# Rotary attention: a tile's three projections traced in one step of the loop, and layer-norm statistics traced over more steps

## The chip, the cores and the metric

The program runs on one core of a Trainium2 chip. The metric is the device time of one execution in microseconds (us), as the median of several runs. The engines are named as in the profile: PE is TensorE's matmul stream, PEld its weight loads, DVE is VectorE, ACT is ScalarE, POOL is GpSimd and SP is SyncE. Each engine works through its own list of instructions in order and waits at semaphores for the others.

## The reference

The whole program is a stack of four pairs of gated layers: a cross-attention-like layer and a feed-forward layer, each applied to a layer norm of the running activations `x` of shape (32, 64, 256), and added back through `tanh` of a gate. All of it is float32 at the interface. The change concerns the last cross-attention layer, `L3_xattn`, which is cut here to what matters:

```python
x = x + jnp.tanh(g_xattn[3]) * _L3_xattn_ref(_layernorm(x), ctx_2048, Wq, bq, Wk, bk, Wv, bv, Wo, bo)

def _L3_xattn_ref(x, c, ...):          # x, c: (32, 64, 256): 64 channels, 256 positions
    q = split_heads(_proj(x, Wq, bq))  # 8 heads of 8 channels
    k = split_heads(_proj(c, Wk, bk))
    v = split_heads(_proj(c, Wv, bv))
    q = _apply_rotary(q_emb, q)        # t * cos(pos) + rot(t) * sin(pos)
    k = _apply_rotary(k_emb, k)
    scores = jnp.einsum('bhtc,bhsc->bhts', q, k) / math.sqrt(K_CH)
    p_attn = jax.nn.softmax(scores, axis=-1)
    out = jnp.einsum('bhts,bhsc->bhtc', p_attn, v)
    return _proj(out.transpose(...).reshape(...), Wo, bo)
```

Keys and values come from the context, queries from the layer norm of `x`.

## The kernel before

The activations stay on the chip in one tile `c.x` of 16 row tiles of 128 x 256. Each row tile holds two of the 32 sequences. `program` runs the eight layers as Python generators, `block0` to `block7`, and interleaves neighbouring ones: a step of one, then a step of the next. Block 6 is the rotary attention. Its first steps, g = 0 to 6, are traced between the last steps of block 5; from g = 7 it runs alone, with `weights7` (which prepares the last layer's weights on PE, ACT and POOL) traced between its steps from g = 60 on. Block 7, the last feed-forward layer, follows.

The order in which things are traced is not the order in which they run. A planner in the framework takes the traced program, treats the place in the trace as a priority, and plans every engine's list by costs that it assumes: an instruction that is ready in its plan may be placed ahead of earlier ones that are not. It also hands out buffers: a tile of a pool waits until an older tile of the same tag has been read for the last time. Block 7's statistics of `x`, for example, stand in VectorE's list through most of block 6, right behind each update of `x`.

Block 6 works in steps g = 0 to 139, four steps for each of the 32 sequences, so eight steps for a row tile. A step does parts of several sequences at different stages:

- `scores(w, p, g)`, in each step. For the sequence `p` that has just begun, a product `pp` of queries and keys (line 1219) of which only the maximum is kept, by a VectorE reduction (`mx`, line 1227). For the sequence `w` that began six steps earlier, the product again as `pw` (line 1211) with the maxima folded into the queries (`qs`), in the other orientation, and its exponential `e` on ScalarE (line 1223).
- `shift` (lines 1196 and 1198), four steps after a sequence began, turns the maxima and makes `qs`.
- `mix` (line 1234), after eight and ten steps, multiplies `e` with the values; `normalise` (lines 1245 to 1249) after eleven divides by the sums; `turn` (line 1254) after thirteen and `finish` (lines 1260 to 1263) after fifteen, once per row tile, apply the output weights and add to `c.x` on POOL.
- `start(i)` makes keys, values and queries of row tile i. `_norm` (line 139) makes the normalised `xn`. Keys: eight matmuls into `pp` (line 1161), two VectorE operations with cosine and sine (`t`, line 1164), then on POOL a sum `k` (line 1170) and two masked copies `kb` (line 1173). Queries: the same matmuls with `xn`, the same two operations, and a sum `q` on POOL (line 1177). Values: matmuls into `pv` (line 1181) and two ScalarE copies into `va` (line 1186).

[...] Two belong to `c.aux`, tag "a", for one-bank tiles. `pair(name)` hands out two-bank tiles: two buffers in the pool `ps2`, and a third, `c.third`, once block 5 has given its banks back; with the third, every third request goes to it. `pw`, `pp` and the key and query projections take a `pair`; `pv` takes a bank of `c.aux`.

For tile i = g // 8 + 1, `start` is a generator that is advanced at the end of three steps: at g % 8 = 1 (norm and keys), 5 (queries) and 7 (values). Tile 0 is made at g = 0 at once.

The layer-norm statistics of four row tiles form one group, `lns`. The first is made ahead of g = 0. Group n is traced from g = 32n - 14: a mean and variance of one tile in each of four steps (`_mean`, lines 98 and 101), and the inverse root (`_inverse`, `_rsqrt`, lines 87 to 108: eleven small VectorE operations, three Newton rounds among them) at once in the fifth.

## Time and profile before

| | |
|---|---|
| Median of 3 runs | 1457.77 us (1457.44 to 1458.16) |
| Profiled execution: time, span | 1453.52 us, 1451.70 us |
| Granted TensorE clock, mean over the span | 0.934 |
| Block 6: first and last score reduction start | 908.53 us, 1264.28 us |
| PE, DVE, ACT, POOL busy in that stretch of 355.7 us | 332.14, 244.09, 163.51, 113.56 us |

The profile is one execution. Its page gives, for each group of instructions, the line of the kernel, the engine, the operation, the tiles that it writes and reads, the busy time with the mean of one in ns, and then the time in which the engine sat idle just before it, with what ended that. The timeline gives instructions in order of time: start, length of the merged group, and in brackets the idle time before it and its releaser. A view of windows gives the busy time of PE, PEld, DVE, ACT and POOL in a stretch, then the granted TensorE clock, the share of DMA and the rate. The ends of matmuls are modelled, so a busy PE is not a PE at its peak; the time from one group's start to the next one's says more.

### The profile page before, as it was taken

How to read it: one execution, taken by the hardware profiler on the slowest of the kernel's cores; microseconds unless marked ns; L12 is line 12 of the kernel's file. 1: busy time of each engine (PE TensorE's matmuls, PEld its weight loads, DVE VectorE, ACT ScalarE, POOL GpSimd, SP SyncE). 2: the span in 40 equal slices, each digit the busy share in tenths (PEclk: the TensorE clock that was granted, in tenths of full speed). 3: DMA queues.
4: the chain of work that ended last, by engine and by line, in shares of the span. 5: the costliest groups of instructions: out<-in, count | busy, mean ns of one | idle time of the engine just before them, and what ended most of it. 6: DMA issues, size and time to landing. Idle time of an engine off the chain costs nothing.

```text
span 1451.7 us, 21390 instructions
## 1 busy us (share of the span) xinstructions
PE 1265.6 (87%) x8342; PEld 745.8 (51%) x8342; DVE 930.1 (64%) x2189; ACT 619.1 (43%) x1044; POOL 448.9 (31%) x466
## 2 busy tenths in 40 slices
PE   1889989999879999778888874899899899999999
PEld 1666445455223677555555552455455455546665
DVE  5679685643378877686888778677776677532111
ACT  2554451312311455566777762255455354531110
POOL 3352442301131323344555455233135332100000
PEclk9999999999999999887998887699899899999999
DMA  5000000100530200000000010200000000000000
GB/s 202 15 7 9 1 1 11 48 0 8 196 116 1 95 1 1 1 1 1 2 1 1 1 60 0 87 2 1 1 2 1 1 1 2 1 0 15 15 15 14
DMA packets 10293, 34.12 MB, mean 24 GB/s; under 512 B 1360, under 2 KB 5968, under 8 KB 8528
## 3 DMA queue, kind: packets, MB, share of 16 engines
q1 hardware_dynamic: 10192, 32.76, 6.3%
q8 instruction: 65, 1.06, 0.3%
q14 instruction: 36, 0.29, 0.1%
HBM read 30.66 MB, written 2.10 MB: 23 GB/s over the span
## 4 chain that ended last, share of the span: by engine, by line
PE 55%; DVE 25%; POOL 9%; issue 4%; ACT 4%; DMA 2%; SPq 0%; POOLq 0%; DVEq 0%; ACTq 0%
PE pw L1211 5%; PE po L1371 4%; PE pg L1361 4%; PE pu L1361 4%; PE pp L1219 4%; PE pc L581 4%; PE po L1234 3%; POOL kb L1173 2%; DVE mx L1227 2%; PE pq L806 2%; PE pu L434 2%; PE pg L434 2%; PE pm L1061 2%; PE pu L437 2%; DMA w<-in_l2f 2%
## 5 line engine op out<-in xcount | busy, mean ns | idle before, releaser
L1223 ACT ACTIVATE e<-pw 128x1024 f32<-128x1024 f32 x128 | 131.0, 1024 | 175.5 <-PE pp L1219 171.5
L1227 DVE TENSOR_REDUCE mx<-pp 128x4 f32<-128x1024 f32 x128 | 156.0, 1219 | 77.4 <-PE pp L1219 77.4
L1211 PE MATMUL pw<-qs,kb 32*128 32x256 f32 x1024 | 159.0, 415 | 7.0 <-DVE mx L1227 7.0
L1219 PE MATMUL pp<-kb,q 32*128 32x512 f32 x512 | 153.7, 676 | 7.5 <-DVE mx L1227 5.0
L1211 PEld LDWEIGHTS pw<-qs,kb 32*128 32x128 f32 x1024 | 88.3, 188 | 49.5 <-issue 26.6
L581 PE MATMUL pc<-xw,wb 64*64 64x512 f32 x768 | 93.3, 619 | 0.2 <-DVE x L514 0.2
L440 ACT ACTIVATE sg<-pg 128x512 f32<-128x512 f32 (+1 forms) x75 | 37.8, 511 | 115.9 <-PE pg L434 50.5
L98 DVE BATCH_NORM_STATS2 ln_st<-x 128x6 f32<-128x256 f32 x128 | 51.0, 411 | 38.2 <-POOL x L1263 27.6
L1364 DVE TENSOR_TENSOR h<-pu,sg 128x512 f32<-128x512 f32 x32 | 22.1, 691 | 80.8 <-PE pu L1361 80.8
L441 DVE TENSOR_TENSOR h<-pu,sg 128x512 f32<-128x512 f32 (+1 forms) x75 | 42.5, 573 | 48.3 <-PE pu L434 30.0
L1234 PE MATMUL po<-e,va 128*32 128x256 f32 x1024 | 70.6, 395 | 1.2 <-ACT e L1223 1.2
L1363 ACT ACTIVATE sg<-pg 128x512 f32<-128x512 f32 x32 | 19.1, 597 | 122.8 <-PE pg L1361 122.7
L732 POOL TENSOR_TENSOR acc<-acc,sq 128x512 f32<-128x512 f32 x28 | 39.4, 1408 | 69.8 <-ACT sq L731 68.4
L581 PEld LDWEIGHTS pc<-xw,wb 64*64 64x64 f32 x768 | 29.8, 138 | 59.6 <-issue 58.8
L1361 PE MATMUL pg<-xf,wa 128*128 128x512 f32 x128 | 60.3, 592 | 0.0
L1361 PE MATMUL pu<-xf,wa 128*128 128x512 f32 x128 | 60.3, 592 | 0.0
L1170 POOL TENSOR_TENSOR k<-t,t 128x512 f32<-128x512 f32 x16 | 20.3, 1266 | 123.4 <-DVE t L1164 123.4
L1371 PE MATMUL po<-hb,h 128*128 128x256 f32 x256 | 55.9, 379 | 0.0
L1066 POOL TENSOR_TENSOR v<-v,wb 128x512 f32<-128x512 f32 x32 | 40.6, 1274 | 42.7 <-ACT v L1065 42.5
L1371 PEld LDWEIGHTS po<-hb,h 128*128 128x128 f32 x256 | 48.6, 190 | 8.3 <-issue 1.9
L139 DVE TENSOR_SCALAR xn<-x,ln_mv,ln_r 128x256 f32<-128x256 f32 x112 | 49.5, 474 | 4.9 <-PE pt L153 4.1
L1219 PEld LDWEIGHTS pp<-kb,q 32*128 32x128 f32 x512 | 41.0, 192 | 22.4 <-DVE mx L1227 16.5
(337 smaller groups left out, 3012.8 us busy)
## 6 DMA issues: line engine op xcount, KB each, us to landing
w<-in_l2f SPq DMA_DIRECT2D x12, 512.0 KB, 4.4
wa<-in_l0f SPq DMA_DIRECT2D x2, 1828.0 KB, 12.2
wa<-in_l1f SPq DMA_DIRECT2D x2, 1536.0 KB, 9.2
wa<-in_l3f SPq DMA_DIRECT2D x2, 1536.0 KB, 8.1
wb<-in_conv SPq DMA_DIRECT2D x1, 2048.0 KB, 7.6
ctx<-in_ctxT SPq DMA_DIRECT2D x2, 1024.0 KB, 6.2
ctx<-in_ctxN SPq DMA_DIRECT2D x2, 1024.0 KB, 6.0
out<-x SPq DMA_DIRECT2D x16, 128.0 KB, 1.7
```

The lines of the kernel that those rows point to most:

```text
L98: ins = c.nc.vector.bn_stats(st, c.x[:, i, :])
L139: c.nc.vector.tensor_scalar(xn, c.x[:, i, :], mv[:, j, 0:1], rs[:, j : j + 1], ALU.subtract, ALU.mult)
L434: nc.tensor.matmul(p, wt[:, k, fc], xf[:, k, :N], start=k == 0, stop=False, skip_group_check=True)
L441: nc.vector.tensor_tensor(h[s][:, f, :], pu, sg, ALU.mult)
L581: nc.tensor.matmul(pcs[h][to], w[rows, k, m, h, :], xw[rows, k, h, :, Z - m : Z - m + 32], start=m == 0, stop=m == Z)
L1211: nc.tensor.matmul(pw[:, jj, k, :], w.k[rows, h, k * P : (k + 1) * P], w.qs[rows, :], start=True, stop=True)
L1219: nc.tensor.matmul(pp[:, jj], p.q[rows, t * P : (t + 1) * P], p.k[rows], start=True, stop=True)
L1223: nc.scalar.activation(e, pw, AF.Exp, scale=scale)
L1227: nc.vector.tensor_reduce(p.mx[:, t, i0 : i0 + 2, 16:18], pp, AX.X, ALU.max, negate=True)
L1234: nc.tensor.matmul(po[strip(j), :], a.v[:, k, 2 * j + h, :], a.e[h, j][:, k, :], start=k == 0, stop=k == 1)
L1361: nc.tensor.matmul(p, wt[:, k, fc], xf[:, k, :], start=k == 0, stop=k == 1)
L1371: nc.tensor.matmul(po, h[:, f, q * P : (q + 1) * P], c.w2h[:, f, :], start=f == 0, stop=f == NH - 1)
```

## The change

`start` now has two parts in place of three. The first, at g % 8 = 1, is the norm of `x` alone. The second, at g % 8 = 3, traces everything else: the eight key matmuls, the value matmuls, the eight query matmuls, then the two ScalarE copies of the values, the two VectorE operations and three POOL operations of the keys, and those of the queries. `pv` is now a `pair` tile, so that the three projections take the three buffers one after the other, a whole turn. The call to `start` also moves inside the step: it stands right behind `scores`, ahead of `mix`, `shift`, `normalise`, `turn` and `finish`.

The inverse root is written as a generator (`_inverse_slowly`, `_rsqrt_slowly`) that stops ahead of each Newton round; `_inverse` and `_rsqrt` run it to its end, for all other callers. In block 6 a new generator `stats6` traces a group's statistics from g = 32n - 18 over eight steps: four means, then the first two operations of the inverse, then one Newton round to a step. The operations and their number are the same.

```diff
@@ block6, start(i)
             xn = _norm(c, tp, lns[i // 4], i, bufs=2)
             ctx = c.ctx.rearrange("p k t -> p (k t)")[:, i * D : (i + 1) * D]
-
-            def project(w, src, n):
+            yield
+
+            def project(w, src):
...
+                return pp
+
+            def rotate(pp, n):
+
                 t = [tp.tile([P, 2, D], F32, tag=f"t{r}", name=f"t{r}") for r in range(2)]
...
-            t = project(wk, ctx, 1)
+            pk = project(wk, ctx)
+            pv = pair("pv").rearrange("p a b d -> p (a b d)")[:, : 2 * P].rearrange("p (j o) -> p j o", j=2)
+            for j in range(2):
+                nc.tensor.matmul(pv[:, j, :], ctx[:, j * P : (j + 1) * P], wv, start=True, stop=True)
+            pq = project(wq, xn)
+            va = vas[i % 3]
+            for n in range(2):
+                src = pv[:, :, n * S : (n + 1) * S].rearrange("p k (h d) -> p k h d", d=HC)
+                nc.scalar.copy(va[:, n, :, :, :HC], src)
+            t = rotate(pk, 1)
             k = tp.tile([P, 2, D], F32, tag="k", name="k", bufs=1)
             nc.gpsimd.tensor_tensor(k, t[0], t[1], ALU.add)
             kb = tp.tile([P, 2, 2, D], F32, tag="kb", name="kb", bufs=3)
             for h in range(2):
                 nc.gpsimd.tensor_scalar(kb[:, :, h, :], k, odd[:, h : h + 1], None, ALU.mult)
-            yield a
-            t = project(wq, xn, 0)
+            t = rotate(pq, 0)
             q = tp.tile([P, 2, D], F32, tag="q", name="q", bufs=3)
             nc.gpsimd.tensor_tensor(q, t[0], t[1], ALU.add)
-            yield a
-            pv = ps1.tile([P, 2, P], F32, tag="a", name="pv")
-            for j in range(2):
-                nc.tensor.matmul(pv[:, j, :], ctx[:, j * P : (j + 1) * P], wv, start=True, stop=True)
-            va = vas[i % 3]
             o = tp.tile([P, 2, 2, S], F32, tag="o", name="o")
...
@@ block6, the steps
+        def stats6(i0):
+            mv = sm.tile([P, 4, 2], F32, tag="ln_mv", name="ln_mv", bufs=2)
+            for j in range(4):
+                _mean(c, sm, mv[:, j, :], i0 + j)
+                yield
+            yield from (None if r is None else (mv, r, i0) for r in _inverse_slowly(c, sm, mv, "ln", 2))
...
             scores(at(6), at(0), g)
+            if g // 8 + 1 < B // 2:
+                if g % 8 == 1:
+                    parts = start(g // 8 + 1)
+                    next(parts)
+                if g % 8 == 3:
+                    seqs += next(parts)
             if a := first(8):
                 mix(a, 0)
...
-            if g // 8 + 1 < B // 2 and g % 8 in (1, 5, 7):
-                if g % 8 == 1:
-                    parts = start(g // 8 + 1)
-                fresh = next(parts)
-                if g % 8 == 7:
-                    seqs += fresh
-
-            ahead = g - 32 * len(lns) + 14
-            if len(lns) < 4 and ahead >= 0:
-                if ahead == 0:
-                    mv = sm.tile([P, 4, 2], F32, tag="ln_mv", name="ln_mv", bufs=2)
-                if ahead < 4:
-                    _mean(c, sm, mv[:, ahead, :], 4 * len(lns) + ahead)
-                else:
-                    lns.append((mv, _inverse(c, sm, mv, "ln", 2), 4 * len(lns)))
+
+            if len(lns) + (more is not None) < 4 and g == 32 * len(lns) - 18:
+                more = stats6(4 * len(lns))
+            if more:
+                ln = next(more)
+                if ln:
+                    lns.append(ln)
+                    more = None
@@ _rsqrt becomes a generator
+def _rsqrt_slowly(c, pool, nv, tag, bufs=1):
...
     for _ in range(3):
+        yield None
         nc.vector.tensor_tensor(t, r, r, ALU.mult)
         nc.vector.tensor_tensor(t, t, nv, ALU.mult)
         nc.vector.scalar_tensor_tensor(r, t, 1.5, r, ALU.add, ALU.mult)
-    return r
+    yield r
```

More of the change, by code (lines that the diff above doesn't have):

```diff
@@ L81, in _rsqrt @@
 def _rsqrt(c, pool, nv, tag, bufs=1):
+    return [r for r in _rsqrt_slowly(c, pool, nv, tag, bufs)][-1]
+def _rsqrt_slowly(c, pool, nv, tag, bufs=1):
     nc = c.nc
@@ L104, in _inverse, with _inverse_slowly @@
 def _inverse(c, pool, mv, tag, bufs=1):
+    return [r for r in _inverse_slowly(c, pool, mv, tag, bufs)][-1]
+def _inverse_slowly(c, pool, mv, tag, bufs=1):
     n = mv.shape[1]
@@ L108, in _inverse @@
     c.nc.vector.tensor_scalar(nv, mv[:, :, 1], 1e-5, -0.5, ALU.add, ALU.mult)
-    return _rsqrt(c, pool, nv, tag, bufs)
+    yield from _rsqrt_slowly(c, pool, nv, tag, bufs)
 def _stats(c, pool, i0=0, n=NT, bufs=1, here=False):
@@ L1173, in start @@
                 nc.gpsimd.tensor_scalar(kb[:, :, h, :], k, odd[:, h : h + 1], None, ALU.mult)
-            yield a
-            t = project(wq, xn, 0)
+            t = rotate(pq, 0)
             q = tp.tile([P, 2, D], F32, tag="q", name="q", bufs=3)
             nc.gpsimd.tensor_tensor(q, t[0], t[1], ALU.add)
-            yield a
-            pv = ps1.tile([P, 2, P], F32, tag="a", name="pv")
-            for j in range(2):
-                nc.tensor.matmul(pv[:, j, :], ctx[:, j * P : (j + 1) * P], wv, start=True, stop=True)
-            va = vas[i % 3]
             o = tp.tile([P, 2, 2, S], F32, tag="o", name="o")
             for n in range(2):
-                src = pv[:, :, n * S : (n + 1) * S].rearrange("p k (h d) -> p k h d", d=HC)
-                nc.scalar.copy(va[:, n, :, :, :HC], src)
                 a[n].q, a[n].k, a[n].v, a[n].o = q[:, n], kb[:, n], va[:, n], o
@@ L1263, in finish @@
             nc.gpsimd.tensor_tensor(c.x[:, a.i, :], c.x[:, a.i, :], y, ALU.add)
+        def stats6(i0):
[4 more added lines that the diff above has]
+            yield from (None if r is None else (mv, r, i0) for r in _inverse_slowly(c, sm, mv, "ln", 2))
         lns = [_stats(c, sm, 0, 4, bufs=2)]
-        seqs = []
+        seqs, more = [], None
         for g in range(4 * B + 12):
```

## The prediction

> **What bounds the kernel now.** The change touches only block 6, so I first looked for its stretch: the 128 score reductions (L1227) start between 908.53 and 1264.28 us, about 356 of the span's 1451.70 us. The page says who waits there (busy and mean, then idle time and its releaser).

> ```profile
> PE 1265.6 (87%) x8342; PEld 745.8 (51%) x8342; DVE 930.1 (64%) x2189; ACT 619.1 (43%) x1044; POOL 448.9 (31%) x466
> L1223 ACT ACTIVATE e<-pw 128x1024 f32<-128x1024 f32 x128 | 131.0, 1024 | 175.5 <-PE pp L1219 171.5
> L1227 DVE TENSOR_REDUCE mx<-pp 128x4 f32<-128x1024 f32 x128 | 156.0, 1219 | 77.4 <-PE pp L1219 77.4
> ```

> ScalarE's exponential and VectorE's reduction both wait for TensorE. So I read the pace. One reduction starts in every step g, eight steps take in one tile, and the VectorE timeline gives the length of a round (start, length of the group, idle time before it). First an undisturbed round with its projections, then the last round, which starts no tile:

> ```profile
> 1164.62 1.22 DVE L1227 TENSOR_REDUCE mx<-pp 128x4 f32<-128x1024 f32 x1 [0.74 <-PE pp L1219]
> ...
> 1172.27 1.22 DVE L1227 TENSOR_REDUCE mx<-pp 128x4 f32<-128x1024 f32 x1 [1.23 <-PE pp L1219]
> 1173.41 0.25 DVE L1247 RECIPROCAL rl<-pn 128x16 f32<-128x16 f32 x1
> 1173.69 0.29 DVE L1249 TENSOR_TENSOR o<-pn,rl 128x128 f32<-128x128 f32 x1
> 1175.26 0.43 DVE L98 BATCH_NORM_STATS2 ln_st<-x 128x6 f32<-128x256 f32 x1 [1.27 <-POOL x L1263]
> ...
> 1175.82 1.19 DVE L1227 TENSOR_REDUCE mx<-pp 128x4 f32<-128x1024 f32 x1
> ...
> 1184.92 1.23 DVE L1227 TENSOR_REDUCE mx<-pp 128x4 f32<-128x1024 f32 x1 [0.74 <-PE pp L1219]
> ...
> 1247.15 1.22 DVE L1227 TENSOR_REDUCE mx<-pp 128x4 f32<-128x1024 f32 x1 [0.73 <-PE pp L1219]
> ...
> 1264.28 1.22 DVE L1227 TENSOR_REDUCE mx<-pp 128x4 f32<-128x1024 f32 x1 [1.07 <-PE pp L1219]
> ```

> The round with projections takes 20.30 us (1184.92 - 1164.62). Without them seven steps take 17.13, or 2.447 each and 19.57 for eight. **All three projections of a tile now cost 0.73 us a round.** Steps are 2.45 long whether TensorE has much or little to do in them: the loop is a chain of latencies over three banks. Scores of step g+1 take the bank whose exponential or reduction of step g has just ended. The TensorE and POOL timelines of the same round show the slack:

> ```profile
> 1167.32 1.13 PE L1161 MATMUL pp<-ctx,wb 64*128 64x256 f32 x8
> 1171.09 0.19 PEld L1219 LDWEIGHTS pp<-kb,q 32*128 32x128 f32 x2 [0.34 <-DVE mx L1227]
> 1172.15 0.66 PE L1245 MATMUL pn<-ident,po_sb 128*128 128x128 f32 x4
> 1172.65 0.60 PE L1260 MATMUL py<-oT,wb 128*128 128x256 f32 x2
> 1174.49 0.73 POOL L1263 TENSOR_TENSOR x<-x,y 128x256 f32<-128x256 f32 x1
> 1182.84 0.61 PE L1181 MATMUL pv<-wb,ctx 128*128 128x128 f32 x4
> ```

> In TensorE time, taken from one group's start to the next one's: scores 1.07 (1168.38 to 1169.45), mix 1.00 (1169.45 to 1170.45), pn 0.50 (1172.15 to 1172.65), py 0.52 (to 1173.17), pv 0.54 (1182.84 to 1183.38). A projection of eight 256-column matmuls is read from its like, eight pw at 1264.74 followed by po at 1265.81: 1.07. Step 1 of eight holds scores and a turn (0.37), step 5 only scores, step 7 scores and pn. These are the steps in which K, Q and V stand now, with 1.0, 1.4 and 0.9 us to spare out of 2.45. Step 3 holds scores, pn and py, 2.09, and has 0.36 to spare.

> **The change, part by part.** The profiled execution took 1453.52 us (span 1451.70 and 1.82 around it); the median of the three runs is 1457.77, 4.25 (0.3%) above. I add the difference to the median.

> *Taken out of steps 1, 5 and 7.* Reductions one apart across step 1 and step 5 are 2.76 and 2.77 us apart (1167.07 to 1169.83, 1177.26 to 1180.03); at 2.45 they give back 0.31 and 0.32. V in step 7 costs nothing (2.45), and the two intervals around the 1.27 us wait make 4.99 instead of 4.90. Together -0.72.

> *Put into step 3.* K, V and Q follow each other there, ahead of pn and py. The work is 1.07 + 1.07 + 0.54 + 1.07 + 0.50 + 0.52 = 4.77 us against 2.45: +2.32. Nothing else covers it, since the next step's scores stand behind it on TensorE. V must wait for the exponential and Q for the reduction of step 3 to give up their banks (about 1.3 us after the scores end), but K's 1.07 and then pn lie in that wait. The next scores need K's bank back: reduction to 1.27, then the two rotations L1164 (1.41 together, from 1168.50) to 2.7 us, while TensorE is busy until 3.7. So no new wait for a bank decides there. The lengths of K and Q are the soft terms: 0.86 each (two row halves side by side, twice the 0.43 between the 0.70 of four and the 1.13 of eight) would make 4.35, and a V that waits with nothing in between 5.0. Net per round 1.6, with ends 1.2 and 1.9.

> *Rounds.* start runs for tiles 1 to 15; tile 1 falls among block 5's work, where two pair buffers serve and the granted clock was 0.50 (908.6 to 929.1 us). Tiles 2 to 15: 14 x 1.6 = +22.4. For tiles 0 and 1, V now takes a pair buffer that it left alone before: between -1 and +3, I take +1 (the wait for a bank is 1.22 at 908.60).

> *POOL, VectorE, ScalarE.* K's three POOL operations (1.27 + 3.10) start two steps later, Q's (1.37) two earlier: one run of 5.7 us after step 3. It ends about 8.5 us after step 3's scores; the tile is needed five steps, over 12 us, later. If POOL is busy with the 8.7 us of weights7 (L1326 and L1327 from 1117.53), that cover is gone, and up to 5 us would show once. The two V copies on ScalarE (0.43) fall behind the exponential, in idle time. But the update x (L1263), traced after all this, may stand behind Q on POOL, and VectorE runs in order: block 7's statistics, which the planner pulls far ahead, already hold it for 1.27 us a round. With x 9 us after step 3 they would hold a reduction by up to 2.6 us, most of it caught up, as now; were x to go ahead of K, 0.1 a round is gained. Ends -0.1 and +1.5; I take +0.2, x 14 = +3, near the row where such a wait was caught up.

> *Statistics.* Same operations, same number. The planner already runs them when VectorE is free in its plan: those traced at g = 86 ran at 1015.5, near g = 37, between two reductions. Other places in the program do not hold them back, so I expect the stall there to remain: 0, with ends -3 (that round took 23.13 instead of 20.30) and +1; I take -2, since VectorE's order around it is dealt anew. No DMA is issued in the moved steps, and nothing passes SP's queue.

> Sum: 22.4 + 1 + 3 - 2 = +24, rounded down to +23 for the soft projection length: 1457.8 + 23 = 1481 us.

> **A rule weighed.** Stalls of a microsecond matter by what they do to TensorE's clock:

> ```profile
> 1016.00:1017.90 1.90, 0.34 (x8) 0.10 (x4) 1.80 (x6) 0.05 (x1) 0.18 (x1) 0.99 0.00 0
> 1017.90:1021.30 3.40, 3.40 (x15) 1.92 (x16) 2.47 (x9) 1.02 (x1) 0.00 (x0) 0.50 0.00 0
> 1217.60:1221.20 3.60, 1.18 (x12) 0.69 (x8) 3.46 (x10) 1.02 (x1) 0.00 (x0) 1.00 0.00 0
> ```

> The third number from the end is the granted clock. A gap of 1.56 us was followed by 3.4 us at half clock; gaps of 1.45 and 0.99 us within one window were not. [...] By the trace one near 1.5 us can also cost 1.7 (3.4 us at half clock). My sum makes no such gap; the second rival does.

> **The rivals.** *Main case (0.58):* +23, or 1470 to 1493 over the ends of the projection length and of the held reductions.

> *Held VectorE (0.15):* x lands behind Q and every round stalls about 1.3 us on top: 22 + 14 x 1.3 = +40, 1498; with half clock after each, 14 x 1.7 more, 1522. For it speaks the 6.74 us TensorE gap before 1134.63, when weights7 made x late. Against it, the 1.27 us held now cost almost nothing.

> *Faster (0.11):* one mechanism, in step 3: the planner drops the projections into the waits for banks of the neighbouring steps, so that a whole turn costs less than the two odd banks do now. It decides from 2.45 + 0.72 = 3.17 us for the interval after step 3. If they became free: -0.72 x 14 = -10, with the statistics stall -13, 1445. For it: L1161 waits on reductions today. Against: 4.77 us of work, and next to nothing to overlap it.

> *Repaid (0.12):* the burst costs its 22, but the 10.2 us that one round lost to the late x (reductions at 1113.80 and 1144.32, 30.51 us) and the statistics stall go: 1465, slower still.

> The spread over more steps doing nothing is in the main case. No change: 0.04.

> **The numbers.** About 0.2%, 3 us, is what a measurement tells from no change. Slower 0.58 + 0.15 + 0.12 = 0.85, same 0.04, faster 0.11. The range 1460 to 1502 leaves out the faster and unchanged cases and the worst of the held ones, about 0.2 together; the main case alone is 1470 to 1493.

> **What would show it.** Right: per round seven intervals of 2.45 and one near 4.8 us, round about 21.9; L1161 and L1181 in one run per tile; TensorE busy through it. Wrong: that interval under 3.2 us, intervals of 2.45 becoming shorter, or rounds that differ by more than 3 us, with half clock (then stalls decide, not work). x later than Q on POOL, and bn_stats before the reduction of step 5, would show the held VectorE. Statistics that run step by step near g = 14, 46 and 78 would show that the planner follows the program after all.

## The result, and the profile after

The changed kernel takes 1519.71 us (median of 6 runs, 1518.19 to 1521.00) against 1456.97 before: ratio 1.0445, 95% interval 1.0424 to 1.0466, slower by about 63 us. The profiled execution has a span of 1516.4 us (1451.7 before) and a mean granted clock of 0.923 (0.934).

The page after: busy time of the engines, then groups with busy time, mean of one, idle time before and its releaser.

```profile
PE 1294.6 (85%) x8342; PEld 751.1 (50%) x8342; DVE 932.3 (61%) x2189; ACT 621.5 (41%) x1044; POOL 446.2 (29%) x466
L1244 DVE TENSOR_REDUCE mx<-pp 128x4 f32<-128x1024 f32 x128 | 156.2, 1220 | 122.4 <-PE pp L1236 122.1
L1240 ACT ACTIVATE e<-pw 128x1024 f32<-128x1024 f32 x128 | 131.0, 1023 | 198.0 <-PE pp L1236 194.1
L1236 PE MATMUL pp<-kb,q 32*128 32x512 f32 x512 | 167.6, 738 | 28.6 <-DVE mx L1244 22.3
L104 DVE BATCH_NORM_STATS2 ln_st<-x 128x6 f32<-128x256 f32 x128 | 51.0, 412 | 52.7 <-POOL x L1280 41.8
```

The counts are those of before: no work was added. TensorE is busy 29 us longer with the same instructions, and VectorE and ScalarE wait longer for it. One row is not about TensorE: the statistics of `x` (L104) waited 41.8 us for POOL's update, against 27.6 before.

Where in the span? The first reduction starts at 907.20 us (908.53 before), and behind the last one both kernels need 187.46 us. Tile 1's round, the eight steps in which its projections are made, takes 26.47 us (30.17 before), the last seven steps 16.85 (17.13). The 14 rounds between, tiles 2 to 15, take 378.4 us against 308.4: **the whole loss, 70 us, is in the rounds of tiles 2 to 15**, 5.0 us in each; the 5.3 us won elsewhere bring it down to the 64.7 by which the two spans differ. Here is an undisturbed round on VectorE (of tile 4), from step 3 on (start, length of the group, idle time before it):

```profile
991.56 1.22 DVE L1244 TENSOR_REDUCE mx<-pp 128x4 f32<-128x1024 f32 x1 [1.08 <-PE pp L1236]
992.70 1.40 DVE L1180 SCALAR_TENSOR_TENSOR t<-pp,wb,con 128x512 f32<-128x512 f32 x2
994.73 1.41 DVE L1180 SCALAR_TENSOR_TENSOR t<-pp,wb,con 128x512 f32<-128x512 f32 x2 [0.63 <-PE pp L1173]
996.06 0.25 DVE L1264 RECIPROCAL rl<-pn 128x16 f32<-128x16 f32 x1
996.23 0.32 DVE L149 TENSOR_SCALAR xn<-x,ln_mv,ln_r 128x256 f32<-128x256 f32 x1
996.46 0.28 DVE L1266 TENSOR_TENSOR o<-pn,rl 128x128 f32<-128x128 f32 x1
999.44 0.43 DVE L104 BATCH_NORM_STATS2 ln_st<-x 128x6 f32<-128x256 f32 x1 [2.70 <-POOL x L1280]
999.90 0.18 DVE L107 BATCH_NORM_AGGREGATE ln_mv<-ln_st 128x2 f32<-128x6 f32 x1
1000.00 1.19 DVE L1244 TENSOR_REDUCE mx<-pp 128x4 f32<-128x1024 f32 x1
...
1006.47 1.22 DVE L1244 TENSOR_REDUCE mx<-pp 128x4 f32<-128x1024 f32 x1 [2.48 <-PE pp L1236]
```

From step 3's reduction (991.56) to step 4's (1000.00) it is 8.44 us, where the prediction had near 4.8. Step 4's scores were done by 996.70; VectorE stood 2.70 us at a statistic of block 7, a layer that starts only some 300 us later, waiting for `x`. ScalarE's `y`, which is added to `x`, and POOL say why `x` was late, and TensorE what the held reduction held:

```profile
995.67 0.56 ACT L1279 ACTIVATE y<-py,gbo,gate 128x256 f32<-128x256 f32 x1 [1.65 <-PE py L1277]
994.24 1.27 POOL L1195 TENSOR_TENSOR k<-t,t 128x512 f32<-128x512 f32 x1 [20.36 <-DVE t L1180]
995.61 3.10 POOL L1198 TENSOR_SCALAR kb<-k,con 128x512 f32<-128x512 f32 x2
998.68 0.72 POOL L1280 TENSOR_TENSOR x<-x,y 128x256 f32<-128x256 f32 x1
999.36 1.27 POOL L1201 TENSOR_TENSOR q<-t,t 128x512 f32<-128x512 f32 x1
```

```profile
996.11 0.59 PE L1236 MATMUL pp<-kb,q 32*128 32x512 f32 x2
1001.58 0.48 PE L1228 MATMUL pw<-qs,kb 32*128 32x256 f32 x2 [2.43 <-DVE qs L1215]
1002.66 1.75 PE L1251 MATMUL po<-e,va 128*32 128x256 f32 x16
```

`y` was done at 996.23, but `x` stood behind K's 4.4 us on POOL and began at 998.68. TensorE then idled 2.43 us, and in the windows of the same round (busy time of PE, PEld, DVE, ACT, POOL; third from the end the granted clock) this follows:

```profile
999.20:1001.60 2.40, 0.02 (x3) 0.03 (x3) 2.12 (x5) 1.02 (x1) 1.43 (x2) 1.00 0.00 0
1001.60:1002.90 1.30, 1.30 (x17) 0.84 (x20) 1.18 (x2) 0.09 (x1) 0.00 (x0) 1.00 0.00 0
1002.90:1006.30 3.40, 3.40 (x28) 1.60 (x20) 1.10 (x1) 1.31 (x2) 0.00 (x0) 0.50 0.02 5
```

After the gap TensorE worked at full clock for 1.3 us, then 3.4 us at half: the mix of L1251 took 1.75 us for its usual 1.07. In the stretch from tile 2's first reduction to the last one, the traces have 79.5 us at half clock, against 21.1 before.

The same steps in an undisturbed round of each kernel that matters below (from one score reduction's start to the next one's, us; step k is the interval after step k's reduction):

| kernel | step 3 | step 4 | step 5 | step 6 | other four | round |
|---|---|---|---|---|---|---|
| before | 3.55 | 1.44 | 2.77 | 2.44 | 10.10 | 20.30 |
| after | 8.44 | 1.44 | 1.33 | 3.70 | 9.58 | 24.49 |
| after, statistics kept out | 5.11 | 2.44 | 2.45 | 2.31 | 9.72 | 22.03 |
| after, `x` on VectorE | 6.23 | 1.44 | 2.34 | 2.46 | 9.58 | 22.05 |
| before, statistics kept out | 2.37 | 2.44 | 2.78 | 2.45 | 10.17 | 20.21 |
| three steps, statistics kept out | 2.37 | 2.44 | 2.78 | 2.45 | 9.96 | 20.00 |

### The profile page after: what moved, and what is told of

The parts are those of the page before. It is cut to its first block, busy times and chain, and to the rows that moved or that the text cites. A ratio compares the mean times of both kernels' runs of the same rounds, so it can differ in the third digit from the quotient of the medians.

```text
span 1516.4 us, 21386 instructions
## 1 busy us (share of the span) xinstructions
PE 1294.6 (85%) x8342; PEld 751.1 (50%) x8342; DVE 932.3 (61%) x2189; ACT 621.5 (41%) x1044; POOL 446.2 (29%) x466
## 4 chain that ended last, share of the span: by engine, by line
PE 54%; DVE 24%; POOL 10%; issue 5%; ACT 4%; DMA 2%; SPq 0%; POOLq 0%; ACTq 0%; DVEq 0%
PE pp L1236 5%; PE pw L1228 5%; PE po L1251 4%; PE po L1394 4%; PE pg L1384 4%; PE pu L1384 4%; PE pc L591 3%; DVE mx L1244 3%; POOL kb L1198 3%; PE pq L816 2%; PE pu L444 2%; PE pu L447 2%; PE pg L444 2%; DMA w<-in_l2f 2%; DVE xn L149 2%
## 5 line engine op out<-in xcount | busy, mean ns | idle before, releaser
L1240 ACT ACTIVATE e<-pw 128x1024 f32<-128x1024 f32 x128 | 131.0, 1023 | 198.0 <-PE pp L1236 194.1
L1228 PE MATMUL pw<-qs,kb 32*128 32x256 f32 x1024 | 181.8, 451 | 26.2 <-DVE qs L1215 26.2
L1236 PE MATMUL pp<-kb,q 32*128 32x512 f32 x512 | 167.6, 738 | 28.6 <-DVE mx L1244 22.3
L1228 PEld LDWEIGHTS pw<-qs,kb 32*128 32x128 f32 x1024 | 98.2, 205 | 74.4 <-issue 30.3
L1195 POOL TENSOR_TENSOR k<-t,t 128x512 f32<-128x512 f32 x16 | 20.3, 1270 | 260.6 <-DVE t L1180 260.6
L104 DVE BATCH_NORM_STATS2 ln_st<-x 128x6 f32<-128x256 f32 x128 | 51.0, 412 | 52.7 <-POOL x L1280 41.8
L1251 PE MATMUL po<-e,va 128*32 128x256 f32 x1024 | 78.5, 430 | 1.2 <-ACT e L1240 1.2
L1236 PEld LDWEIGHTS pp<-kb,q 32*128 32x128 f32 x512 | 43.9, 208 | 50.0 <-DVE mx L1244 30.5
L1251 PEld LDWEIGHTS po<-e,va 128*32 128x32 f32 x1024 | 28.7, 117 | 60.6 <-issue 43.8
```

The lines of the kernel that those rows point to most:

```text
L104: ins = c.nc.vector.bn_stats(st, c.x[:, i, :])
L1228: nc.tensor.matmul(pw[:, jj, k, :], w.k[rows, h, k * P : (k + 1) * P], w.qs[rows, :], start=True, stop=True)
L1236: nc.tensor.matmul(pp[:, jj], p.q[rows, t * P : (t + 1) * P], p.k[rows], start=True, stop=True)
L1240: nc.scalar.activation(e, pw, AF.Exp, scale=scale)
L1251: nc.tensor.matmul(po[strip(j), :], a.v[:, k, 2 * j + h, :], a.e[h, j][:, k, :], start=k == 0, stop=k == 1)
```

## The experiments

**The theory and its rival.** Call the three projections that now stand together the burst. Theory: two losses lie on each other, the burst's own work on TensorE, near +23 us as predicted, and a hold, in which block 7's statistics, planned far ahead into block 6, stop VectorE until POOL has updated `x`; half clock follows from the hold. Rival: the burst is the whole loss, by its waits and the half clock that it brings, and the waiting statistic is a by-product.

**1. The statistics kept out of block 6, after and before.** An argument of the helper keeps an instruction at its place in the trace, so block 7's statistics run in block 7.

```diff
@@ block7, features(t)
-            pts = _normT(c, sm, c.aux, _stats(c, sm, 4 * t, 4, bufs=2), t, "a")
+            pts = _normT(c, sm, c.aux, _stats(c, sm, 4 * t, 4, bufs=2, here=True), t, "a")
```

> The changed kernel with the same pin of block 7's statistics. 'Held VectorE': only the burst is left, about 1.6 us a round over the pinned kernel before, 14 x 1.6 = 22 us: about 1465 us, with the interval behind step 3 near 5 us instead of 8.4, and hardly any half clock between 940 and 1250 us. 'Burst': 1515 to 1520 us as without the pin, the interval stays at 8.4.

> The kernel before, with one change: block 7's statistics of x (bn_stats) are pinned behind what is traced ahead of them on VectorE, so that they can no longer stand in VectorE's list in the middle of block 6 and wait there for the update x on POOL. Theory 'held VectorE' (the list of VectorE stops at a bn_stats whose x is late, and score reductions behind it are late): the round of 30.5 us and the one of 25.5 us become ordinary, the others stay at 20.3; 10 to 20 us faster than before, about 1442 us. Theory 'burst' (the loss of the changed kernel is TensorE work and bank waits where the projections stand together, the held statistics only fill idle time): no difference from before, within 3 us.

Measured: after 1472.93 us (ratio to the kernel before 1.0133, 1.0108 to 1.0158), before 1444.73 (0.9928, 0.9903 to 0.9954). The 14 rounds take 320.1 and 294.0 us, half clock 7.7 and 7.4 us; behind the last reduction 199.1 and 197.6 us instead of 187.5, since the statistics are now done there, and TensorE runs 17.1 and 13.7 us at half clock there against none (after) and 0.4 (before). So among the 14 rounds' 70 us **the burst is 320.1 - 294.0 = 26.1 us, and the hold with its half clock 43.9**: 58.3 after (378.4 - 320.1) against 14.4 before (308.4 - 294.0). The same round on TensorE, without the hold, shows the burst itself:

```profile
1171.21 1.14 PE L1173 MATMUL pp<-ctx,wb 64*128 64x256 f32 x8
1172.52 0.71 PE L1187 MATMUL pv<-wb,ctx 128*128 128x128 f32 x4 [0.18 <-ACT e L1240]
1173.16 1.13 PE L1173 MATMUL pp<-xn,wb 64*128 64x256 f32 x8
1174.23 0.66 PE L1262 MATMUL pn<-ident,po_sb 128*128 128x128 f32 x4
1174.72 0.60 PE L1277 MATMUL py<-oT,wb 128*128 128x256 f32 x2
1175.25 0.48 PE L1228 MATMUL pw<-qs,kb 32*128 32x256 f32 x2
```

From start to start: K 1.31, V 0.64, Q 1.07, pn 0.49, py 0.53, and 1.07 for scores make the 5.11 us of the table. K's 1.31 holds the one wait, V's for the exponential.

**2. The update of `x` ahead of the burst's POOL work.** `finish` is traced right behind `scores`, ahead of `start`, in the changed kernel.

```diff
             scores(at(6), at(0), g)
+            if (a := first(15)) and a.n:
+                finish(a)
...
-            if (a := first(15)) and a.n:
-                finish(a)
```

> The changed kernel with finish traced ahead of start in the step, nothing pinned: the update x goes onto POOL ahead of k and kb of the same step. 'Held VectorE': x lands some 4 us earlier, the bn_stats behind it no longer hold the reduction, and about 40 of the 63 us come back: 1475 to 1485 us. 'Burst': the same matmuls stand together, 1515 to 1520 us.

Measured: 1489.55 us (1.0237, 1.0221 to 1.0253). `x` is first on POOL now (1194.74, `k` at 1197.38), and 33 of the 58 us go from the 14 rounds (345.2), less than expected: the planner moves the statistic along, ahead of the rotation of K, where it waits 1.21 us for `x` and delays the release of K's bank. The interval is 6.08, undisturbed rounds 22.5 us; three rounds still take about 30.

**3. The burst at step 5 in place of 3.**

```diff
-                if g % 8 == 3:
+                if g % 8 == 5:
                     seqs += next(parts)
```

> The changed kernel with all three projections in step 5 of eight instead of step 3. Step 5 has no mix, normalise and finish behind it, and 1.4 us to spare. 'Held VectorE': x has no K in front of it on POOL, so nothing is held, and the burst is 1.07 + 2.68 = 3.75 us against 2.45, +1.3 - 0.72 = +0.6 a round: about 1466 us. 'Burst' in the sense of bank waits at any place: well above 1490 us.

Measured: 1476.89 us (1.0151, 1.0131 to 1.0171). The burst now makes an interval of 4.81 at step 5, more than the 3.75 expected: V waits 0.26 us for a reduction, and Q's rotation and `xn` stand on VectorE ahead of the next one. But `x` no longer meets `kb`: the statistic waits 0.76 us, step 3 takes 3.03, an undisturbed round 21.7, and half clock falls to 27.8 us. The same work moved two steps away from `finish` gives 43 us back.

**4. Block 7's statistics inside block 6, at a place of our choice.** Each tile's mean is fixed two steps behind its `finish` instead of being kept out, in both kernels, to save the 10 us behind block 6.

```diff
@@ block6, the steps (and block7, which uses these means)
+            if (a := first(17)) and a.n:
+                c.stat7(a.i)          # _mean(c, sm, mvs[a.i // 4][:, a.i % 4, :], a.i, here=True)
```

> The kernel before, with block 7's mean and variance of a row tile traced and pinned in block 6, two steps after the finish of that tile (step 5 of eight), instead of in block 7. By then x has landed, so VectorE never waits for it, and block 7 does not have to make the statistics at its start, where the pin alone cost about 10 us (the time from the last score reduction to the end grew from 187.5 to 197.6 us). 'Held VectorE': block 6 as in the pinned kernel, tail nearly as before: 1435 to 1442 us, faster than both kernels. If the tail grew for another reason (block 7's inverse and norms late, a cold clock): 1445 us or more.

> The changed kernel with the same move of block 7's statistics. 'Held VectorE plus burst': 1.8 us a round over the kernel of e7, as between the two pinned kernels (22.04 against 20.21 us): 1460 to 1468 us. If the pin acted by something else than x being awaited: above 1480.

Measured: before 1460.61 us (1.0051, 1.0032 to 1.0069), a clear miss; after 1469.44 (1.0114, 1.0077 to 1.0151), just above what was expected. Behind block 6 it is 188.07 and 188.05 us. In the changed kernel undisturbed rounds stay at 22.04; the three with an inverse root take 0.3 to 3.8 us more. In the kernel before, the place chosen is where Q is projected: the statistic stands ahead of Q's rotation, step 5 becomes 3.31, and in the three rounds in which the planner puts the inverse root of a finished group of block 7 behind it, ahead of the same rotation, it becomes 6.45, 8.94 and 6.15. A place that is free in one version is not free in the other.

**5. V in a bank of c.aux again, with the burst, statistics kept out.**

```diff
-            pv = pair("pv").rearrange("p a b d -> p (a b d)")[:, : 2 * P].rearrange("p (j o) -> p j o", j=2)
+            pv = ps1.tile([P, 2, P], F32, tag="a", name="pv")
```

> The changed kernel, pinned as in e3, with the values' matmuls back in a bank of the one-bank pool, so that no whole turn of the three pair buffers is taken. 'Burst is TensorE work': only V's wait for the exponential (0.25 us) can go, 0 to 5 us faster than e3: 1468 to 1473. 'The turn of the banks decides': a change of over 10 us either way.

Measured: 1466.76 us (1.0088, 1.0060 to 1.0117), 6 less than with the pair, with intervals that overlap. An undisturbed round takes 21.79 us for 22.04, the 14 rounds 315.3 for 320.1: in these two profiles 4.8 us is the price of V's place in the whole turn of the banks. The two profiles differ more behind block 6 (191.8 and 199.1 us), where the one with the pair had its 17.1 us at half clock and this one none; no run says whether that comes from V.

**6. The projections apart again, statistics kept out.** Keys at step 1, queries at 5, values at 7, each traced right behind `scores`; V stays in a pair.

```diff
                 if g % 8 == 1:
                     parts = start(g // 8 + 1)
                     next(parts)
-                if g % 8 == 3:
+                    next(parts)
+                if g % 8 == 5:
+                    next(parts)
+                if g % 8 == 7:
                     seqs += next(parts)
```

> The changed kernel, pinned as in e3, with the projections taken apart again: keys in step 1, queries in step 5, values in step 7, but still traced right behind the scores, and the values still in a pair buffer. 'Togetherness costs, since a step has 1 us to spare and the three need 2.7': the round falls back to 20.2 us, 1445 us, as the pinned kernel before. 'The place ahead of mix, or V in the pair buffers, costs': it stays above 1460.

Measured: 1435.72 us (0.9877, 0.9848 to 0.9906): 37 us less than with the burst, and about 1.2% faster than the kernel before. An undisturbed round takes 19.4 to 20.0 us, about what eight steps without any projection take (19.57, the prediction's own count). VectorE in the same part of such a round, steps 3 and 4:

```profile
1149.39 1.23 DVE L1246 TENSOR_REDUCE mx<-pp 128x4 f32<-128x1024 f32 x1 [1.09 <-PE pp L1238]
1150.53 0.25 DVE L1266 RECIPROCAL rl<-pn 128x16 f32<-128x16 f32 x1
1150.81 0.29 DVE L1268 TENSOR_TENSOR o<-pn,rl 128x128 f32<-128x128 f32 x1
1151.76 1.22 DVE L1246 TENSOR_REDUCE mx<-pp 128x4 f32<-128x1024 f32 x1 [0.66 <-PE pp L1238]
```

No statistic stands between, and no rotation: 2.37 us.

**7. The same three steps, statistics free.** The experiment before with `here=True` taken away.

> The projections of a tile apart again (keys at step 1, queries at 5, values at 7, V in a pair, traced right behind scores), block 7's statistics free to run ahead as in the changed kernel. Theory (the hold is a consequence of the burst, which fills POOL and VectorE ahead of the update of x): holds of about the size of the kernel before, so 1440 to 1465 us, rounds 20 to 21, half clock in block 6 under 30 us. Rival (the hold comes from where start now stands in the step, or from V's pair buffer): holds of 2.4 us and half clock remain in most rounds, 1475 to 1495 us.

Measured: 1450.44 us (0.9961, 0.9946 to 0.9975). Step 3 is 3.49 or 3.64 in undisturbed rounds, as before the change, and half clock 20.0 us. `start` stands where the change put it, V is in a pair, and the statistics may run ahead: the projections no longer stand together, nor K's POOL work ahead of `x` in the step of `finish`, and 69 us go. With the statistics kept out it was 37. The other 32 us are what the burst in that step does to the hold; experiment 3, where the burst stays whole, shows that the place in that step matters.

**8. The update of `x` on VectorE.** The changed kernel with one word changed; burst and free statistics stay.

```diff
@@ block6, finish
-            nc.gpsimd.tensor_tensor(c.x[:, a.i, :], c.x[:, a.i, :], y, ALU.add)
+            nc.vector.tensor_tensor(c.x[:, a.i, :], c.x[:, a.i, :], y, ALU.add)
```

> The changed kernel with one edit: the update of x runs on VectorE in place of POOL; burst and free statistics stay. Theory (a statistic hoisted ahead of a reduction holds VectorE because POOL hands over x 2.4 us late, behind k and kb): the statistic finds x done, VectorE now waits only for y, the hold falls from 2.4 us to about 0.5, interval after step 3 from 8.4 to 5.1-6.0, 1470 to 1492 us. Rival (the burst alone, or its half clock, makes the loss, and the late x is a by-product): within 8 us of 1520.

Measured: 1474.52 us (1.0147, 1.0119 to 1.0174), 45 us less, with VectorE doing more. The round again on VectorE:

```profile
989.35 1.41 DVE L1180 SCALAR_TENSOR_TENSOR t<-pp,wb,con 128x512 f32<-128x512 f32 x2 [0.63 <-PE pp L1173]
990.68 0.25 DVE L1264 RECIPROCAL rl<-pn 128x16 f32<-128x16 f32 x1
990.89 0.42 DVE L1280 TENSOR_TENSOR x<-x,y 128x256 f32<-128x256 f32 x1
991.23 0.28 DVE L1266 TENSOR_TENSOR o<-pn,rl 128x128 f32<-128x128 f32 x1
991.43 0.51 DVE L149 TENSOR_SCALAR xn<-x,ln_mv,ln_r 128x256 f32<-128x256 f32 x1
991.87 0.41 DVE L104 BATCH_NORM_STATS2 ln_st<-x 128x6 f32<-128x256 f32 x1
992.31 0.18 DVE L107 BATCH_NORM_AGGREGATE ln_mv<-ln_st 128x2 f32<-128x6 f32 x1
992.41 1.19 DVE L1244 TENSOR_REDUCE mx<-pp 128x4 f32<-128x1024 f32 x1
993.52 0.41 DVE L1215 TENSOR_TENSOR qs<-pt,q 128x256 f32<-128x256 f32 x1
```

The statistic is still ahead of step 4's reduction, in its old place, and waits for nothing. The groups of the stretch from 934 to 1252 us, first of the changed kernel, then of this one, say it in one number, the idle time ahead of the statistics:

```profile
L104 DVE BATCH_NORM_STATS2 ln_st<-x 128x6 f32<-128x256 f32 x11 | 4.7, 427 | 30.8 <-POOL x L1280 30.8
```

```profile
L104 DVE BATCH_NORM_STATS2 ln_st<-x 128x6 f32<-128x256 f32 x12 | 4.9, 410 | 0.0
```

The reduction is 1.1 us late, and steps 3 and 4 together take 7.67 us against 7.55 with no statistics there at all: caught up. Half clock is 27.4 us. The rival falls here: the burst stays as it was, and most of the loss goes. Of the hold's 58.3 us in the 14 rounds, 43.4 go with the wait for POOL alone (335.0 for 378.4). The other 14.9 lie in the rounds of tiles 6, 10, 11 and 14: in 6, 10 and 14 a group of block 7 is complete, and its inverse root, eleven operations, stands on VectorE around step 4's reduction.

**9. Two attempts to improve on experiment 6:** V back in c.aux (the edit of experiment 5), and the first group of block 7's statistics set free (`here=t > 0`).

> The three steps apart and block 7's statistics kept out of block 6 (1435.7 us), and V again in a bank of c.aux as before the change. Theory (V's pair costs only where it must wait for the exponential inside the burst): the same within 3 us, 1433 to 1439. Rival (taking V out of the three pair buffers helps everywhere, as it did by 6 us with the burst): 1427 to 1432.

> The three steps apart; of block 7's statistics only the first group (tiles 0 to 3) may run ahead into block 6, groups 1 to 3 stay behind it. Theory (keeping the statistics out costs about 10 us behind block 6, a quarter of it or more for the first group, whose x is ready from about tile 3's finish on, while a hold needs a statistic placed right behind a late x): tail about 3 to 5 us shorter, holds in at most four rounds: 1430 to 1436 us. Rival (the freed statistics are again placed right behind the updates of x of the first four tiles and hold VectorE there): 1438 to 1446.

Measured: 1443.04 us (0.9924, 0.9903 to 0.9944) and 1439.71 us (0.9898, 0.9879 to 0.9916). Both miss what the theory had expected; the second lies where its rival had it, with the freed statistics holding VectorE again. V in c.aux costs nothing to speak of later (rounds 19.9), but tile 1's round takes 30.17 us in place of 23.29: with two pair buffers and block 5 beside it, the order there comes out otherwise; why is open. The free group saves 8.0 us behind block 6 (189.7) and loses more in front: tile 1's round takes 27.80, four of the next five have holds, and block 6 as a whole takes 11.4 us longer (337.7 for 326.3). Experiment 6 stays the fastest.

**The spread of the inverse root** needs no run: the planner's instruction lists of all engines are the same, entry for entry, with and without that part, in either kernel. The trace agrees: the last group, now traced from g = 78 on, has its inverse root at 1024.4 us, ahead of the reduction of g = 36, where the kernel before had it at 1015.5, near g = 37.

## Why the prediction was right or wrong

*Direction and the burst: right.* The largest term, 14 x 1.6 = +22.4, was measured as 26.1, 1.86 a round. The predicted round of 21.9 us is 22.03 where the hold is absent. The interval came out at 5.11 for 4.77: V's wait for the exponential was not filled as the text had it (0.18 us left inside K's 1.31), V took 0.64 for 0.54, and the projection length 1.07 for Q held. K's place between scores and V was right; pn did not move into the wait.

*Tiles 0 and 1: small.* Predicted +1, measured -3.7 in tile 1's round and -1.3 ahead of it; the ends -1 to +3 missed it.

*Statistics: the reason right, the gain not.* "Other places in the program do not hold them back" holds to the letter: the lists with and without that part are identical. The -2 taken on top of it, for an order dealt anew, had no ground.

*The held VectorE: the step that failed.* The sum took +0.2 a round, +3 in all, with an end of +1.5, on the ground that a held reduction is caught up. It measured 43.9 us, 3.1 a round. Three links of that step were wrong:

- *Where `x` stands on POOL.* The text had "behind Q" as what may be, and priced it low. `x` stood ahead of Q, but behind `k` and `kb`, and 4.4 us of K's work were enough: it ended at 999.40, and without them it could have ended near 997.0 (`y` done at 996.23, 0.72 for `x`).
- *Which reduction is held.* The text looked for a statistic ahead of step 5's reduction. It stood ahead of step 4's, the very one that the burst had already delayed. The planner's list is made for its assumed costs and keeps its order on the chip, whether or not the wait is short there: VectorE stood 2.70 us at the statistic, while step 4's scores were done by 996.70.
- *"Most of it caught up, as now".* This was half true, and its failure made the size. In the round shown, the hold adds 8.44 - 5.11 = 3.33 us; steps 4 and 5 win back 1.00 and 1.12. Then half clock takes 1.39 in step 6 (3.70 for 2.31). Over the 14 rounds, 14 x 1.2 = 17 us remain of such a hold after catching up; the 52.1 us of half clock that go with the wait (79.5 - 27.4) lose up to half of that, 26 us, where TensorE is busy throughout. Together 43, an estimate from these numbers, near experiment 8's 43.4. The 14.9 us of the rounds with an inverse root and the one behind them are not in it; the kernel before lost 14.4 us in rounds of the same kind, so what the change added is about the price of the wait for POOL.

*The gap and the clock.* From the trace's gap of 1.56 us and the 3.4 us of half clock behind it the text took that a gap near 1.5 us can also cost 1.7 us. That was right, and then it went unused: "My sum makes no such gap". The changed kernel's trace has eleven TensorE gaps of over 2.3 us in the 14 rounds and the last steps, seven of them between 2.31 and 2.62, four longer (4.01, 4.20, 4.95, 5.81), and half clock begins during or within 2 us of every one. The length of a gap alone does not tell it, as the last section shows.

*The rivals.* "Held VectorE" had the mechanism, and with half clock in each round the size, 1522 us against 1519.7; the agreement is partly luck, since the hold was larger and the half clock less regular than written. It was given 0.15, because "the 1.27 us held now cost almost nothing". That evidence was read from undisturbed rounds: keeping the statistics out of the kernel before shows that they cost it 14.4 us already, all of it in the rounds of tiles 6, 10 and 14 (4.5, 8.0 and 2.2), those with an inverse root; in tile 10's weights7 had also made `x` late. How much of that was waiting is not separated. The range ended at 1502, inside this rival's own span of 1498 to 1522.

*What to have read.* All of it was in the trace of before. The statistic waited for POOL in nearly every round (1.27 us), `y` to `x` was its last link, and the change puts 4.4 us of POOL work directly ahead of that link. The prediction counted POOL's work against the tile's need, five steps later, and not against the one wait that was already exposed.

## What to carry to other kernels

Before moving work on to a second engine's queue, look for the instruction on any in-order engine that already waits for that queue, even if it is off the critical path and needed only much later: it can become the bound as soon as its operand is late (here VectorE, 2.70 us in the round shown), and work of low priority that a planner pulled forward is the first suspect. Spread work that fits into the slack of separate steps; gathered into one step it costs all by which it exceeds that step's slack, here 26 us. A hold that looks as if it is caught up should be priced with the clock that follows it, here 1.39 us in step 6 of that round.

## What the runs showed of the hardware

```profile
1014.45:1017.87 3.42, 1.86 (x28) 0.79 (x24) 3.25 (x12) 1.33 (x2) 1.38 (x1) 1.00 0.00 0
1017.87:1021.28 3.41, 3.41 (x15) 1.93 (x16) 2.50 (x9) 1.02 (x1) 0.00 (x0) 0.50 0.00 0
1215.83:1219.24 3.41, 1.96 (x24) 1.04 (x18) 3.06 (x12) 1.83 (x3) 0.01 (x1) 1.00 0.00 0
1219.24:1222.65 3.41, 2.42 (x28) 1.51 (x32) 3.34 (x8) 0.18 (x1) 0.09 (x1) 1.00 0.00 0
1222.65:1226.06 3.41, 3.41 (x38) 1.97 (x30) 2.18 (x3) 2.23 (x5) 1.19 (x1) 1.00 0.00 0
```

The window with 1.86 us of work was followed by half clock. From 1217.6 to 1221.2 TensorE was idle longer, 2.42 of 3.60 us, but the boundary at 1219.24 divides that time: the windows on its two sides hold 1.96 and 2.42 us of work, and the clock stayed full. In the two profiles, from tile 2's first reduction to the last one, all 13 full-clock windows with at most 1.40 us of work were followed by half clock, one of the three with 1.84 to 1.96 us, and none of the 165 with 2.21 us or more. Half clock ended after 15 of the 18 half-clock windows in which TensorE was busy throughout, and after none of the 11 with at most 3.22 us of work. Busy times rest on modelled ends, so these are near values, and they are counts of two profiles: a window with 1.84 us was followed by full clock and one with 1.86 us by half, so they show no line between the two.

An update of 128x256 on POOL took 0.72 us (after, at 998.68) where VectorE took 0.42 (experiment 8, at 990.89), but what mattered was the queue, with 4.4 us of K's work ahead of it, not the length.
